# Register-addressed column copies: 24 a step on VectorE and on ScalarE, addresses in four parts, three operand blocks

## The chip, the cores and the metric

The kernel runs on one core of a Trainium2 chip. The metric is the device time of one execution in microseconds (us). A core has a matrix engine (TensorE, PE in the profile; PEld is its weight load), VectorE (DVE), ScalarE (ACT), GpSimd (POOL) and SyncE (SP). Each engine has a sequencer that reads its instructions in order and hands them to the engine; rows of the profile with a q behind the engine's name (DVEq, ACTq) are instructions that the sequencer carries out itself, such as loading registers from memory. Engines wait for each other by semaphores. Matrix results land in PSUM, from where VectorE or ScalarE take them; everything else works in SBUF, 128 partitions wide.

## The reference

One layer of a graph network on 12,500 nodes and 212,500 edges, sorted by destination, in float32; then a residual addition and a layer norm:

```python
msg_in = jnp.concatenate([nodes[row], nodes[col], edge_features], axis=-1)
messages = _mlp(msg_in, mW1, mb1, mW2, mb2)          # relu(x @ W1 + b1) @ W2 + b2
aggregated = jax.ops.segment_sum(messages, col, num_segments=nodes.shape[0])
upd_in = jnp.concatenate([nodes, aggregated], axis=-1)
x = _layernorm(x + _mlp(upd_in, uW1, ub1, uW2, ub2), axis=-1)
```

Node features are 64 wide, edge features 32, hidden layers 128. `row` is the source of an edge, `col` its destination.

## The kernel before

Edges go in 554 groups (G) of 384 (GE, three tiles of 128). Since edges are sorted, a group's destinations lie in a window of 32 nodes. One step of the main loop (L718) works on three groups at once, in a pipeline, all of it one run of TensorE instructions that waits once, at its first, and signals once, at its last:

- `turn` of group k (L423) transposes the group's gathered source features and its one-hot matrix of destinations (`own_s`, 128 x 96) into PSUM. ScalarE evacuates that into the operand block `own_st` (L440).
- `hidden` of group k - 2 (L448) multiplies `own_st`, which also holds the edge features, with weights and the window's projected destinations (`own_wm`). ScalarE applies the ReLU (L464).
- `sums` of group k - 4 (L474) sums the messages by destination. VectorE adds them to `own_agg` (L495) and the counts to a row of `own_xc` (L496), at a column that a register gives.

PSUM buffers alternate by k, so TensorE's step k + 2 waits for what ScalarE and VectorE did after step k.

The source features come in two ways. Most groups are **gathered**: GpSimd issues three indirect DMAs a group (L184), 16 steps ahead, into a ring of 20 buffers; a gather waits for ScalarE's evacuation of the group that had the buffer, and for copies of that step. The other groups (the table COPIED) are **copied**: all nodes also lie transposed in SBUF (`own_xc`, a node is a column of 64 partitions), and VectorE and ScalarE copy one column after another to the group's place in `own_st`, in the steps ahead of the group's own. Each copy is an instruction of 64 x 4 bytes (L599 on VectorE, L601 on ScalarE) whose address stands in a register. Copying starts at step 18 (BEGIN). COLS columns a step are copied, so a copied group is ready every 384 / COLS steps.

The addresses lie in SBUF as whole numbers, eight steps' worth a buffer (`index`, made by L563). `registers(k, part)` (L565) makes the load into registers (TENSOR_LOAD, L578), `fetch(part)` (L585) the copies that use them. VCOLS and ACOLS give the parts: before, VectorE has parts of 12 and 8, ScalarE one of 16. The order in which these calls stand in the loop is the order on each engine:

- VectorE's load of 12 stands right ahead of the additions (called from `add` by way of the list `between`), its copies of 12 behind them; then come the one-hot of group k + 6 (L412), the load of 8 and the copies of 8.
- ScalarE's load of 16 for step k + 1 stands behind the copies of step k, thus ahead of step k + 1's evacuation and ReLU; the 16 copies come behind the ReLU.
- Every fourth step, VectorE also loads 4 registers with the columns of the sums (L371).

`own_st` has four blocks (BLOCKS) of four groups. `inputs(b)` (L355) has SyncE load a block's edge features (192 KB); it waits for the step that last read the block, as does the first copy of a group on each engine (L603).

Some 23 times, when a stretch of 512 nodes has all its sums, an `update` of those nodes runs through the steps in six parts (L500 to L548): two products, a ReLU, two products, statistics and scaling.

Of the kernel before, what the change touches and what calls it, by code (L numbers as in the profile page):

```python
# [32 lines left out]
G = (E + GE - 1) // GE  # L33
SB = 4
AHEAD = 16
RING = AHEAD + 4
BLOCKS = 4
NW = 2 * SB
COUNT = 96
NH = 3  # L40
# [9 lines left out]
TIMES = 4  # L50
BEGIN = 18
CHECKED = 8
VCOLS = (12, 8)
ACOLS = (16,)
COLS = sum(VCOLS + ACOLS)
SPAN = 8
STREAMS = ()
# [4 lines left out]
def tiles_of(g):  # L62

    n = min(GE, E - g * GE)
    return [min(P, n - j * P) for j in range((n + P - 1) // P)]
# [27 lines left out]
for _, rate, _ in STREAMS:  # L93
    BY_ROWS.append([])
    while True:
        last = BEGIN + (P * (len(BY_ROWS[-1]) + 1) - 1) // rate + ROW_LEAD
# [7 lines left out]
class Own:  # L104
# [4 lines left out]
    def __init__(self, nc, ctx):  # L109
        def on(name, *shape, of=nc.sbuf_tensor):  # L110
            return ctx.enter_context(of(name, list(shape), F32)).ap()

        self.s = [on(f"own_s{i}", P, TG, D + W) for i in range(RING)]
        self.st = [on(f"own_st{i}", P, SB * GE) for i in range(BLOCKS)]
        self.wm = [on(f"own_wm{i}", P, H) for i in range(NW)]
# [14 lines left out]
def ordered(ctx: ExitStack, tc: tile.TileContext, a, own, ok):  # L130
# [28 lines left out]
    def after(first, *others):  # L159

        tc.declare_no_dep(first.ins, group="quiet", reason="waits for the last of a step")
        for i in others:
            tc.add_manual_dep(
                first.ins, i.ins.name,
                mybir.DependencyInfo(mybir.DependencyClass.Sync, mybir.DependencyReason.DATA),
                reason="the kernel's own rings",
            )
        return first
# [73 lines left out]
    def bit(k):  # L242

        nodes = [NEAR_NODES + (N - NEAR_NODES) * i // BITS for i in (k, k + 1)]
        tiles = [first + (NT - first) * i // BITS for i in (k, k + 1)]
        nc.sync.dma_start(src_sb[:, slice(*tiles)], a["src"][:, slice(*tiles)])
        nc.sync.dma_start(xc[:D, slice(*nodes)], a["xT"][:, slice(*nodes)])
        rest(nodes[0], nodes[1] if k < BITS - 1 else NP)

    def zeroed(k):  # L250

        n0, n1 = (NP * i // BITS for i in (k, k + 1))
        nc.vector.memset(agg[:, n0:n1], 0.0)
# [101 lines left out]
    def inputs(b):  # L355
        if b * SB >= G:
            return
        c0, c1 = b * SB * GE, min(E, (b + 1) * SB * GE)
        efs_by[b] = nc.sync.dma_start(own.st[b % BLOCKS][D + W :, : c1 - c0], a["efT"][:, c0:c1])
        after(efs_by[b], *([hidden_by[(b - BLOCKS + 1) * SB - 1]] if b >= BLOCKS else []))  # L360

    def columns(g):
        t, c = own.st[g // SB % BLOCKS], (g % SB) * GE
        return t, c, sum(tiles_of(g))
# [13 lines left out]
    def projected(c):  # L378

        base, n = TABLE[c]  # L380
        ps = ups.tile([H, CH], F32, name="u_ps").rearrange("p (n h) -> p n h", n=4)
        for j in range(n):
            nc.tensor.matmul(ps[:, j], xc[: D + 1, base + j * P :][:, :P], w1b,  # L383
                             start=True, stop=True)
        t = rowp.tile([P, 4, H], F32, name="t")
        nc.scalar.activation(t[:, :n], ps[:, :n], AF.Copy)  # L386
        written.append(after(nc.sync.dma_start(
            by_dst[base : base + n * P, :].rearrange("(n p) h -> p n h", n=n), t[:, :n])))
# [34 lines left out]
    def turn(g, ps):  # L423
# [11 lines left out]
        def copy(step):  # L435
# [4 lines left out]
                after(nc.scalar.activation(t[r, c : c + n], xt[r, :n], AF.Copy), step))]  # L440
            if g >= BLOCKS * SB:
                after(copies[0], hidden_by[g - BLOCKS * SB])
            copy_by[g] = copies
# [30 lines left out]
    def sums(g, ps):  # L474
        h, s = own.h[g % NH], own.s[g % RING]
        sizes = tiles_of(g)
        sg = ps[2][:, : TIMES * W].rearrange("p (t w) -> p t w", w=W)
        counted = ps[2][0:1, TIMES * W :][:, :W]
        did = []
        for j, p in enumerate(sizes):  # L480
            did.append(nc.tensor.matmul(  # L481
                sg, h[:p, j, :],
                s[:p, j, D:].unsqueeze(1).to_broadcast([p, TIMES, W]),
                start=j == 0, stop=j == len(sizes) - 1))
        for j, p in enumerate(sizes):
            did.append(nc.tensor.matmul(counted, own.one[:p], s[:p, j, D:],  # L486
                                        start=j == 0, stop=j == len(sizes) - 1))

        def add(step):
            sums_by[g] = step  # L490
            at = bass.ds(starts.pop(g), W)
            count = xc[COUNT : COUNT + 1, at]
            if between:
                between.pop()()
            a = after(nc.vector.tensor_tensor(agg[:, at], sg[:, 0, :], agg[:, at], ALU.add), step)  # L495
            return [a, after(nc.vector.tensor_tensor(count, counted, count, ALU.add), step)]  # L496

        return did, [*relu_by[g], *copy_by[g]], add
# [60 lines left out]
    def addresses(i):  # L559

        if i in indices:
            t = indices[i][:, : min(SPAN * COLS, GE * len(COPIED) - i * SPAN * COLS)]
            nc.vector.tensor_scalar(t, t, 4.0, float(own.at), ALU.mult, ALU.add)  # L563

    def registers(k, *parts):  # L565

        i, n = divmod(k - BEGIN, SPAN)
        if i < 0:
            return
        all_parts = [*((ET.DVE, c) for c in VCOLS), *((ET.Activation, c) for c in ACOLS)]  # L570
        for part in parts:
            engine, count = all_parts[part]
            c0 = (k - BEGIN) * COLS + sum(c for _, c in all_parts[:part])
            count = min(count, GE * len(COPIED) - c0)
            if count <= 0:
                return
            b = c0 - i * SPAN * COLS
            _, v = nc.values_load_multi_w_load_instructions(  # L578
                indices[i][0:1, b : b + count], engines=[engine],
                min_val=own.at, max_val=own.at + 4 * (N - 1),  # L580
                skip_runtime_bounds_check_because="a source is one of the nodes",
            )
            held[part] = engine, c0, v
# [129 lines left out]
    for n in range(len(STREAMS)):  # L713
        row_indexes(n, 0)
    made = summed = 0
    between, held, last = [], {}, {}

    for k in range(G):  # L718
        if k < BITS:
            bit(k)  # L720
            if k + 2 < BITS:
                zeroed(k + 2)
        if 1 < k < len(TABLE):
            projected(k)
        if k == CHECKED:
            addresses(0)
            for n in range(len(STREAMS)):
                row_addresses(n, 0)
            combined()
            ordered_edges()  # L730
            early.close()
            up = ctx.enter_context(tc.tile_pool(name="upd", bufs=2))
        if k % SB == 2:
            inputs(k // SB + 2)
        if k % SB == 1:
            places(k // SB + 1)
        if k < G - SHORT:
            between.append(lambda: registers(k, 0))
            step((turn, k), *([(hidden, k - 2)] if k > 1 else []),
                 *([(sums, k - 4)] if k > 3 else []))  # L740
            made, summed = max(0, k - 1), max(0, k - 3)
            if between:
                between.pop()()
        else:

            step((turn, k))
            for _ in range(2):
                if summed < made:
                    step((sums, summed))
                    summed += 1  # L750
            for _ in range(2):
                if made <= k:
                    step((hidden, made))
                    made += 1
            registers(k, 0)
        fetch(0)
        window(k + SB)
        for n in range(len(STREAMS)):
            row_numbers(n, k)
            row_fetch(n)  # L760
        onehot(k + LEAD)
        marks_by[k] = [copy_by[k][-1]]
        if k < G - 1:
            for part in range(1, len(VCOLS + ACOLS)):
                if part != len(VCOLS):
                    registers(k, part)
                fetch(part)
                if part >= len(VCOLS) and ET.Activation in last:
                    marks_by[k].append(last[ET.Activation])
            if k + 1 < G - 1:  # L770
                registers(k + 1, len(VCOLS))
            if k >= BEGIN and (k - BEGIN) % SPAN == 0:
                indexes((k - BEGIN) // SPAN + 1)
            if k >= BEGIN and (k - BEGIN) % SPAN == SPAN - 2:
                addresses((k - BEGIN) // SPAN + 1)
        if k + AHEAD < G:
            gather(k + AHEAD)
# [333 lines left out]
```

## Time and profile before

| | |
|---|---|
| median of 3 runs | 1914.63 us (1913.1 to 1914.86) |
| the profiled execution | 1914.16 us |
| its span, first to last instruction | 1912.4 us |
| granted TensorE clock, mean | 0.972 |
| busy: PE, PEld | 1324.3 us (69%), 1170.6 us (61%) |
| busy: DVE, ACT, POOL | 1251.4 us (65%), 1325.2 us (69%), 1431.7 us (75%) |

Times with a decimal point in views of the trace are us from the span's start. In the waits, "A <- B" says that A's engine stood idle until B released it; the numbers are us in total, the count, and the longest. In a timeline the columns are start, duration (of a merged row, up to its last end), engine, line, operation, tiles, shape and count, and in brackets the idle time ahead of it. In views of one line, three numbers with slashes are the shortest, the median and the longest duration in ns.

### The profile page before, as it was taken

To read this page: it belongs to the slowest core of one execution; us is meant where nothing else is said; L and a number is where in the kernel's file an instruction comes from. 1 tells how busy PE (TensorE), PEld (TensorE's weight loads), DVE (VectorE), ACT (ScalarE), POOL (GpSimd) and SP (SyncE) were. 2 spreads that over 40 slices of the span, in tenths; PEclk is the share of its full clock that TensorE was granted. 3 is DMA by queue.
4 is the path that set the end of the run, shared out by engine and by line. 5 is a ranking of instruction groups with operands and counts; after the bars stand their busy time and mean duration, and the time that the engine had idled before them with its cause. 6 is when DMAs were issued, how large, how long until landed. Compare 5 with 4: busy or idle time off the path is not lost. (4 is left out here: it accounts for less than half of the span.)

```text
span 1912.4 us, 56586 instructions
## 1 busy us (share of the span) xinstructions
PE 1324.3 (69%) x12323; PEld 1170.6 (61%) x12323; DVE 1251.4 (65%) x12584; ACT 1325.2 (69%) x9559; POOL 1431.7 (75%) x1521
## 2 busy tenths in 40 slices
PE   5877777767767766676666776766766766667677
PEld 4766666666656655665655665655656655556566
DVE  4347777766666666676766766666667666676662
ACT  4468787766767767776767776776676677676662
POOL 7777777777777777777777777777777777777774
PEclk9889999989999999999999999999999999999998
DMA  5532222222222222222222212222222222222221
GB/s 141 139 97 64 53 50 52 49 49 48 45 53 52 46 52 48 49 49 48 53 48 48 50 44 53 52 46 52 48 50 48 51 47 52 45 53 48 49 50 25
DMA packets 113836, 105.15 MB, mean 55 GB/s; under 512 B 52115, under 2 KB 83488, under 8 KB 113488
## 3 DMA queue, kind: packets, MB, share of 16 engines
q0 software_dynamic: 48448, 49.68, 13.6%
q1 hardware_dynamic: 64196, 51.29, 9.7%
q8 instruction: 104, 1.70, 0.4%
q14 instruction: 244, 2.00, 0.3%
q10 hardware_dynamic: 844, 0.48, 0.1%
HBM read 91.68 MB, written 9.62 MB: 53 GB/s over the span
## 5 line engine op out<-in xcount | busy, mean ns | idle before, releaser
L184 POOL DMA_INDIRECT own_s<-in_x,src_sb x1514 | 1430.9, 945 | 462.5 <-issue 261.5
L599 DVE COPY own_st<-own_xc 64x4 uint8 x10460 | 896.5, 191 | 27.7 <-DMA by_dst<-t 3.5
L601 ACT ACTIVATE own_st<-own_xc 64x4 uint8 x8356 | 847.3, 195 | 2.9 <-DMA by_dst<-t 2.9
L429 PE MATMUL own_ps<-own_ident,own_s 128*96 128x128 f32 x1661 | 289.0, 284 | 540.4 <-DMA own_s<-in_x,src_sb 355.6
L440 ACT ACTIVATE own_st<-own_ps 96x384 f32<-96x384 f32 (+1 forms) x554 | 268.6, 485 | 506.7 <-PE own_ps L486 483.7
L429 PEld LDWEIGHTS own_ps<-own_ident,own_s 128*96 128x96 f32 x1661 | 164.3, 129 | 602.0 <-ACT own_h L464 445.0
L481 PE MATMUL own_ps<-own_s,own_h 128*128 128x128 f32 x3322 | 478.6, 282 | 1.3 <-ACT own_h L464 0.6
L495 DVE TENSOR_TENSOR own_agg<-own_ps,own_agg 128x32 f32 x554 | 106.3, 192 | 567.1 <-PE own_ps L486 386.4
L453 PE MATMUL own_ps<-own_wm,own_st 128*128 128x128 f32 x3322 | 476.5, 281 | 0.0
L481 PEld LDWEIGHTS own_ps<-own_s,own_h 128*128 128x128 f32 x3322 | 431.1, 198 | 2.8 <-ACT own_h L464 1.6
L453 PEld LDWEIGHTS own_ps<-own_wm,own_st 128*128 128x128 f32 x3322 | 428.6, 197 | 1.3 <-issue 0.5
L464 ACT ACTIVATE own_h<-own_ps 128x384 f32<-128x384 f32 x553 | 264.8, 479 | 21.2 <-PE own_ps L453 20.0
L486 PE MATMUL own_ps<-own_s,own_one 128*1 128x32 f32 x3322 | 189.1, 194 | 0.0
L486 PEld LDWEIGHTS own_ps<-own_s,own_one 128*1 128x1 f32 x3322 | 113.8, 83 | 69.4 <-issue 5.7
L412 DVE TENSOR_TENSOR own_s<-iota,dlc 128x96 f32<-128x96 f32 x554 | 137.3, 248 | 0.7
L496 DVE TENSOR_TENSOR own_xc<-own_ps,own_xc 1x32 f32 x554 | 102.1, 184 | 31.9 <-PE u_ps L507 13.2
L383 PE MATMUL u_ps<-w1b,own_xc 65*128 65x128 f32 x196 | 31.8, 310 | 32.0 <-DMA own_xc<-in_xT 12.7
L383 PEld LDWEIGHTS u_ps<-w1b,own_xc 65*128 65x128 f32 x196 | 26.8, 211 | 35.0 <-issue 20.3
L519 PE MATMUL u_ps<-same,own_xc 65*128 65x64 f32 (+1 forms) x196 | 39.5, 283 | 0.4 <-ACT u L512 0.4
L386 ACT ACTIVATE t<-u_ps 128x512 f32<-128x512 f32 (+1 forms) x25 | 14.7, 588 | 36.2 <-DMA by_dst<-t 20.0
L521 PE MATMUL u_ps<-u,u 128*128 128x64 f32 (+1 forms) x196 | 38.2, 277 | 0.0
L519 PEld LDWEIGHTS u_ps<-same,own_xc 65*128 65x128 f32 (+1 forms) x196 | 29.9, 192 | 2.5 <-ACT u L512 1.0
(60 smaller groups left out, 264.4 us busy)
## 6 DMA issues: line engine op xcount, KB each, us to landing
own_st<-in_efT SPq DMA_DIRECT2D x138, 192.0 KB
own_s<-in_x,src_sb POOLq DMA_INDIRECT x1514
own_wm<-by_dst SPq DMA_DIRECT2D x554, 16.0 KB
by_dst<-t SPq DMA_DIRECT2D x24, 256.0 KB
out<-o SPq DMA_DIRECT2D x24, 128.0 KB
own_xc<-in_xT SPq DMA_DIRECT2D x12, 179.2 KB
index<-in_src_copied SPq DMA_DIRECT2D x65, 1.1 KB
dlc_i<-in_dst_cols SPq DMA_DIRECT2D x1, 807.0 KB
```

The source lines that it names most:

```text
L184: nc.gpsimd.indirect_dma_start(out=s[:p, j, :D], out_offset=None, in_=x[:, :], in_offset=bass.IndirectOffsetOnAxis(ap=src_sb[:p, g * TG + ...
L412: places_by[g] = nc.vector.tensor_tensor(own.s[g % RING][:, :, D:], iota.unsqueeze(1).to_broadcast([P, TG, W]), dlc[:, g * TG : (g + 1) * ...
L429: nc.tensor.transpose(xt[:, j * P : j * P + p], sides[g] if g in sides and j == TG - 1 else s[:p, j, :], ident[:p, :p])
L440: after(nc.scalar.activation(t[r, c : c + n], xt[r, :n], AF.Copy), step))]
L453: nc.tensor.matmul(pre[:p, j, :], t[:, c + j * P : c + j * P + p], wm[g % NW], start=True, stop=True)
L464: relu_by[g] = [nc.scalar.activation(h, pre, AF.Relu)]
L481: did.append(nc.tensor.matmul(sg, h[:p, j, :], s[:p, j, D:].unsqueeze(1).to_broadcast([p, TIMES, W]), start=j == 0, stop=j == len(sizes) - 1))
L486: did.append(nc.tensor.matmul(counted, own.one[:p], s[:p, j, D:], start=j == 0, stop=j == len(sizes) - 1))
L495: a = after(nc.vector.tensor_tensor(agg[:, at], sg[:, 0, :], agg[:, at], ALU.add), step)
L496: return [a, after(nc.vector.tensor_tensor(count, counted, count, ALU.add), step)]
L599: by[engine] = nc.vector.tensor_copy(o, x_at)
L601: by[engine] = nc.scalar.activation(o, x_at, AF.Copy)
```

## The change

Both engines copy 24 columns a step (COLS 48 instead of 36), and both take their addresses in parts of 12, 4, 4 and 4. VectorE's load of 12 moves behind the additions; ScalarE's first load is now that of the same step and stands behind the ReLU. `own_st` has three blocks.

```diff
-BLOCKS = 4
+BLOCKS = 3
...
-VCOLS = (12, 8)
-ACOLS = (16,)
+VCOLS = (12, 4, 4, 4)
+ACOLS = (12, 4, 4, 4)
...
             count = xc[COUNT : COUNT + 1, at]
-            if between:
-                between.pop()()
             a = after(nc.vector.tensor_tensor(agg[:, at], sg[:, 0, :], agg[:, at], ALU.add), step)
...
-    between, held, last = [], {}, {}
+    held, last = {}, {}
...
         if k < G - SHORT:
-            between.append(lambda: registers(k, 0))
             step((turn, k), *([(hidden, k - 2)] if k > 1 else []),
                  *([(sums, k - 4)] if k > 3 else []))
             made, summed = max(0, k - 1), max(0, k - 3)
-            if between:
-                between.pop()()
         else:
...
-            registers(k, 0)
+        registers(k, 0)
+        if k < G - 1:
+            registers(k, len(VCOLS))
         fetch(0)
         window(k + SB)
...
-            if k + 1 < G - 1:
-                registers(k + 1, len(VCOLS))
```

VectorE in a plain step of the middle of the program, before; the row without names (ISA) computes the address of the addition behind it, and TENSOR_LOAD is a load of addresses:

```order
L578 TENSOR_LOAD index
L495 ISA
L495 TENSOR_TENSOR own_agg<-own_ps,own_agg 128x32
L496 ISA
L496 TENSOR_TENSOR own_xc<-own_ps,own_xc 1x32
L599 COPY own_st<-own_xc 64x4 x12
L412 TENSOR_TENSOR own_s<-iota,dlc 128x3x32
L578 TENSOR_LOAD index
L599 COPY own_st<-own_xc 64x4 x8
```

The same place in the changed program, from the addition on (line numbers are two lower there):

```order
L493 TENSOR_TENSOR own_agg<-own_ps,own_agg 128x32
L494 ISA
L494 TENSOR_TENSOR own_xc<-own_ps,own_xc 1x32
L576 TENSOR_LOAD index
L597 COPY own_st<-own_xc 64x4 x12
L412 TENSOR_TENSOR own_s<-iota,dlc 128x3x32
L576 TENSOR_LOAD index
L597 COPY own_st<-own_xc 64x4 x4
L576 TENSOR_LOAD index
L597 COPY own_st<-own_xc 64x4 x4
L576 TENSOR_LOAD index
L597 COPY own_st<-own_xc 64x4 x4
```

The first load, of 12, now stands behind the two additions and right ahead of its copies; three loads of 4 have taken the place of one of 8.

ScalarE in a plain step, before, from one load to the next:

```order
L578 TENSOR_LOAD index
L440 ACTIVATE own_st<-own_ps 96x384
L464 ACTIVATE own_h<-own_ps 128x384
L601 ACTIVATE own_st<-own_xc 64x4 x16
L578 TENSOR_LOAD index
```

And in the changed program:

```order
L440 ACTIVATE own_st<-own_ps 96x384
L464 ACTIVATE own_h<-own_ps 128x384
L576 TENSOR_LOAD index
L599 ACTIVATE own_st<-own_xc 64x4 x12
L576 TENSOR_LOAD index
L599 ACTIVATE own_st<-own_xc 64x4 x4
L576 TENSOR_LOAD index
L599 ACTIVATE own_st<-own_xc 64x4 x4
L576 TENSOR_LOAD index
L599 ACTIVATE own_st<-own_xc 64x4 x4
```

The load that stood ahead of the evacuation, where ScalarE waits for TensorE, now stands behind the ReLU, and is of 12; the other 12 addresses come in three parts of 4, each right ahead of its copies.

## The prediction

> **What bounds the kernel now.** I read the page first, for the engines' busy time and the costliest groups; then the table of waits, since no engine is busy throughout; then the timeline of the two engines in question.
>
> ```profile
> span 1912.4 us, 56586 instructions
> ...
> L184 POOL DMA_INDIRECT own_s<-in_x,src_sb x1514 | 1430.9, 945 | 462.5 <-issue 261.5
> ```
> ```profile
> DVE own_agg L495 <- PE own_ps L486: 386.4, 324, 6.7
> ...
> POOL own_s L184 <- issue: 261.5, 858, 0.3
> POOL own_s L184 <- DMA own_s<-in_x,src_sb: 173.7, 570, 0.3
> DVE own_agg L495 <- DVE own_st L599: 77.4, 130, 1.0
> ```
> ```profile
> 1063.67 0.94 POOL L184 DMA_INDIRECT own_s<-in_x,src_sb  x1 [0.30 <-issue]
> 1064.92 0.94 POOL L184 DMA_INDIRECT own_s<-in_x,src_sb  x1 [0.30 <-DMA own_s<-in_x,src_sb]
> ```
>
> GpSimd is busy for 75% only, yet it never pauses longer than 0.3 us: that is its fixed distance between two gathers, whatever name stands at it. So a gather costs (1430.9 + 462.5) / 1514 = 1.25 us, and all of them cost 1893 us of a span of 1912.4. **The gathers are the bound.** VectorE waits mostly for TensorE, which waits for gathers. But in 130 steps VectorE waited for nothing but its own last copies, with nothing running on it. That row is where the change will hurt. Here is such a step, from one addition to the next:
>
> ```profile
> 1062.15 0.19 DVE L495 TENSOR_TENSOR own_agg<-own_ps,own_agg 128x32 f32 x1 [0.90 <-DVE mv L529]
> 1062.37 0.18 DVE L496 TENSOR_TENSOR own_xc<-own_ps,own_xc 1x32 f32 x1
> 1062.59 0.94 DVE L599 COPY own_st<-own_xc 64x4 uint8 x12
> 1063.44 0.24 DVE L412 TENSOR_TENSOR own_s<-iota,dlc 128x96 f32<-128x96 f32 x1
> 1063.61 0.68 DVE L599 COPY own_st<-own_xc 64x4 uint8 x8
> 1064.85 0.19 DVE L495 TENSOR_TENSOR own_agg<-own_ps,own_agg 128x32 f32 x1 [0.55 <-DVE own_st L599]
> ```
> ```profile
> L578 DVEq TENSOR_LOAD <-index x2: 593/720/846, 1062.8 to 1063.7; - x2
> ```
>
> The second view is that of the line that loads addresses, in this one step: a load of 8 registers at 1062.8 takes 0.593 us, one of 12 at 1063.7 takes 0.846 us. It ends at 1064.55, and the addition behind it starts at 1064.85, although the copies had been handed out long before. The sequencer does nothing else while it loads. The step lasts 2.70 us with only some 2.0 us of work on the engine: **VectorE's floor is its sequencer**, and 0.593 + 0.846 = 1.44 us of it are loads. Today gathers leave room above that floor.
>
> **The change part by part.** *Fewer gathers.* 48 columns a step instead of 36 make 65 copied groups of 384 instead of 49. That removes 48 gathers; at 1.25 us they are worth 60 us. In a loaded step GpSimd then needs 3 x (1 - 48/384) x 1.25 = 3.28 us. The copies last 65 x 384 / 48 = 520 steps instead of 49 x 384 / 36 = 523. Whoever takes longer than 3.28 us a step becomes the new bound.
>
> *VectorE.* Its loads go from 12 + 8 to 12 + 4 + 4 + 4, its copies from 20 to 24. What a load of 4 more costs can be read, because every fourth step has one (L371, the addresses of the sums):
>
> ```profile
> L371 DVEq TENSOR_LOAD <-start_i x139: 340/343/812, 10.5 to 1882.2; - x139
> ```
> ```profile
> 1150.21 0.19 DVE L495 TENSOR_TENSOR own_agg<-own_ps,own_agg 128x32 f32 x1 [1.01 <-DVE own_st L599]
> ...
> 1153.34 0.19 DVE L495 TENSOR_TENSOR own_agg<-own_ps,own_agg 128x32 f32 x1 [0.97 <-DVE own_st L599]
> ```
> ```profile
> L371 DVEq TENSOR_LOAD <-start_i x1: 347/347/347, 1151.8 to 1151.8; - x1
> ```
>
> This step has that load, again VectorE waited for itself alone, and it lasts 3.13 us: 0.43 more than 2.70, for a load of 0.347. So in a plain step:
> - the load of 8 becomes one of 4: 0.593 - 0.343 = 0.25 less;
> - two more loads of 4: 2 x 0.43 = 0.86 more;
> - four more copies handed over: in the step above 8 of them lie between the end of the load at 1062.8 + 0.593 and the next load at 1063.7, so at most 0.3 / 8 = 0.04 each, part of which is the pause between two loads. I take 0.03, so 0.12; the bounds are 0 and, if 20 copies had made up all of 2.70 - 1.44, 0.25;
> - the load of 12 moves from ahead of the addition to behind it. It stays in the same chain: 0.
>
> The last point needs the question whether the sequencer can run the load while the addition still waits for TensorE. The nearest rows are at the start, on ScalarE:
>
> ```profile
> 12.12 0.60 ACT L386 ACTIVATE t<-u_ps 128x512 f32<-128x512 f32 x1 [2.16 <-PE u_ps L383]
> 12.12 0.47 ACTq L301 DMA_DIRECT2D w2t<-in_mW2T  x1
> ```
>
> The sequencer's own instruction starts only when the activation ahead of it has stopped waiting. So the load begins with the addition at the earliest. Queued behind it are the 24 copies and the one-hot of the step; the next addition comes behind all of those. TensorE waits for the addition two steps on.
>
> Plain step: 2.70 - 0.25 + 0.86 + 0.12 = **3.43 us**. Per step come on top: 0.43 / 4 = 0.11 for L371; and VectorE's share of the updates and of the address arithmetic:
>
> ```profile
> L543 DVE TENSOR_SCALAR o<-u_ps,mv,rstd 128x64 f32<-128x64 f32 (+1 forms) x98 | 27.0, 337 | 1.0
> L563 DVE TENSOR_SCALAR index<-index 1x288 int32<-1x288 int32 x66 | 22.2, 336 | 0.1
> L528 DVE BATCH_NORM_STATS2 stats<-u_ps 128x6 f32<-128x64 f32 (+1 forms) x98 | 20.4, 208 | 5.3 <-PE u_ps L521 5.3
> L529 DVE BATCH_NORM_AGGREGATE mv<-stats 128x2 f32<-128x6 f32 (+1 forms) x98 | 17.8, 182 | 3.5
> ```
>
> L528 and L529 stand in the chain, 38 us; of L543's 27 I count 10, as a load can run beside them: 48 / 520 = 0.09. L563 runs every eighth step, 0.336 / 8 = 0.04, half of it beside loads: 0.02. The average is 3.43 + 0.11 + 0.09 + 0.02 = **3.65 us**, above GpSimd's 3.28. The bound moves from GpSimd to VectorE, and GpSimd will wait for ring space.
>
> *ScalarE* gets 24 copies for 16, and its load of 16 in front becomes 12 behind the ReLU and three of 4.
>
> ```profile
> 1066.12 0.49 ACT L440 ACTIVATE own_st<-own_ps 96x384 f32<-96x384 f32 x1
> 1066.51 0.48 ACT L464 ACTIVATE own_h<-own_ps 128x384 f32<-128x384 f32 x1
> 1066.88 1.62 ACT L601 ACTIVATE own_st<-own_xc 64x4 uint8 x16
> 1068.48 0.49 ACT L440 ACTIVATE own_st<-own_ps 96x384 f32<-96x384 f32 x1
> ```
> ```profile
> L578 ACTq TENSOR_LOAD <-index x523: 313/1021/1340, 90.2 to 1852.7; - x175
> ```
>
> Evacuation and ReLU take 0.76, 16 copies 1.60, so 0.10 each; 16 registers take 1.02, the shortest load (4, the last one) 0.313, so 12 take about 0.78. If the load starts with the evacuation, copies begin at 0.9 and the step takes 0.9 + 2.4 = 3.3; the short loads run beside the copies ahead of them. If it starts only with the ReLU (0.39) and each short load shows 0.1, it is 3.8. I take 3.3, which is nearest to the rows of L386 and L301: no cost, hidden under VectorE's 3.65; without that cover it would be 0.02 over GpSimd's 3.28.
>
> *TensorE* has the same work in a step, about 2.1 us:
>
> ```profile
> 1063.04 0.53 PE L429 MATMUL own_ps<-own_ident,own_s 128*96 128x128 f32 x3
> ...
> 1064.85 0.34 PE L486 MATMUL own_ps<-own_s,own_one 128*1 128x32 f32 x6
> ```
>
> *Three operand blocks.* The edge load on SP (L359) waits for a step one before the step that issues it instead of five before, and the first column of a group waits for a step two back. The landed data is needed eight steps later, some 28 us; that hides it at no cost. Were it late by 1 us each time, 139 loads would cost 139 us.
>
> **Sum.** Loaded stretch before, by the copies' first and last start:
>
> ```profile
> L599 DVE COPY own_st<-own_xc x10460: 148/156/424, 99.1 to 1857.2; 64x4 uint8 x198
> ```
>
> That is 1758 us for 523 steps, 3.36 each. The profiled execution took 1914.2 us; 156 of it lie outside the stretch. Outside come three more steps at ScalarE's shortest period of 2.36 (7 us), less the waits for the last gathers, which now land long before:
>
> ```profile
> 1860.72 0.51 PE L429 MATMUL own_ps<-own_ident,own_s 128*96 128x128 f32 x3 [1.39 <-DMA own_s<-in_x,src_sb]
> ...
> 1894.31 0.50 PE L429 MATMUL own_ps<-own_ident,own_s 128*96 128x128 f32 x3 [1.58 <-DMA own_s<-in_x,src_sb]
> ```
>
> These are the first and the last of five, 5 us in all. That leaves 158. Inside: 520 x 3.65 = 1898. Together **2056 us**, 142 above the profiled execution, which is 0.5 below the median of 1914.63. I give 2055.
>
> **Rivals.**
> - *The loads hide* (12 in 100). If copies can be handed on while a load runs, VectorE's step falls to its own work, 24 copies at 0.07 and the additions, some 2.3 us. GpSimd stays the bound, and 48 gathers less give 1914 - 60 = **1854**. For it: GpSimd never waits today. Against it: 77.4 us of VectorE waiting for itself, and the 0.43 for one more load. [...]
> - *ScalarE becomes the bound* (10 in 100), if its load starts with the ReLU: some 3.75 a step, 520 x 3.75 + 158 = **2108**. It decides above 3.65.
> - *The edge loads come late* (2 in 100): 2055 + 139, near **2190**. SP's queue behind a waiting L359 also holds the windows of four steps on.
>
> **How the numbers follow.** The forecast has 76 in 100. Its unknown terms give, all low (copies handed over for nothing, updates 0.03), 3.45 a step and 1952; all high (0.25, 0.13, 0.04), 3.84 and 2155. Not all lie at one end, so I take 1960 to 2140, which also holds the ScalarE case. A measurement here can tell about 0.2%, 4 us. Faster than that: the first rival, 12 in 100. Slower: 86. Within: 2, should the loads hide in part.
>
> **What would show it.** Right: GpSimd waits far over 0.3 us for ScalarE's copies or the transposes; VectorE's additions wait for L599's copies (now L597) instead of for TensorE, about 3.4 us apart in plain steps; between additions there is a gap ahead of the first copy and ahead of each set of four. Wrong: gathers still 1.25 us apart throughout; or ScalarE without idle time and VectorE waiting for TensorE.

## The result and the profile after

| | before | after |
|---|---|---|
| median | 1913.99 us (1913.1 to 1914.86, 4 runs) | 2067.63 us (2063.42 to 2072.74, 4 runs) |
| ratio | | 1.0804, 95% interval 1.0779 to 1.0829 |
| profiled execution, span | 1914.16 us, 1912.4 us | 2072.74 us, 2070.9 us |
| granted TensorE clock | 0.972 | 0.943 |

The change makes the kernel 8% slower. The page after, its head and the costliest groups of the three engines in question (busy time, mean ns of one, idle time ahead of them):

```profile
span 2070.9 us, 65565 instructions
...
L184 POOL DMA_INDIRECT own_s<-in_x,src_sb x1466 | 1385.0, 945 | 612.1 <-ACT own_st L440 188.3
L597 DVE COPY own_st<-own_xc 64x4 uint8 x12480 | 1118.9, 187 | 469.5 <-issue 440.2
L599 ACT ACTIVATE own_st<-own_xc 64x4 uint8 x12480 | 1249.4, 193 | 47.1 <-DVE own_xc L494 38.3
```

The table of waits after (total us, times, longest in us):

```profile
DVE own_st L597 <- issue: 440.2, 909, 1.1
PEld own_ps L429 <- ACT own_h L464: 408.3, 254, 2.7
...
POOL own_s L184 <- ACT own_st L440: 188.3, 228, 4.1
POOL own_s L184 <- issue: 184.6, 604, 0.4
POOL own_s L184 <- ACT own_st L599: 164.8, 401, 1.5
ACT own_st L440 <- PE own_ps L486: 153.0, 178, 9.2
...
DVE own_agg L493 <- PE own_ps L486: 62.3, 36, 7.0
```

There are 48 gathers less, as the change promised, but GpSimd now pauses up to 4.1 us for ScalarE, where no pause between gathers was over 0.3 us before. VectorE's wait for TensorE fell from 386.4 us to 62.3 us. Its idle time stands ahead of its own copies, with "issue" as its cause: the engine waits for its own sequencer. A plain step on VectorE after, and the view of the address loads in that step:

```profile
1060.87 0.19 DVE L493 TENSOR_TENSOR own_agg<-own_ps,own_agg 128x32 f32 x1
1061.09 0.18 DVE L494 TENSOR_TENSOR own_xc<-own_ps,own_xc 1x32 f32 x1
1062.01 1.02 DVE L597 COPY own_st<-own_xc 64x4 uint8 x12 [0.74 <-issue]
1062.94 0.24 DVE L412 TENSOR_TENSOR own_s<-iota,dlc 128x96 f32<-128x96 f32 x1
1063.11 0.66 DVE L597 COPY own_st<-own_xc 64x4 uint8 x8
1063.94 0.38 DVE L597 COPY own_st<-own_xc 64x4 uint8 x4 [0.17 <-issue]
1064.23 0.18 DVE L493 TENSOR_TENSOR own_agg<-own_ps,own_agg 128x32 f32 x1
```
```profile
L576 DVEq TENSOR_LOAD <-index x4: 341/344/847, 1061.1 to 1063.5; - x4
```

The step lasts 3.36 us instead of 2.70. Between the additions and the first copy VectorE stands idle for 0.74 us while its sequencer loads 12 registers for 0.847 us. The second addition has 0.18 us of work to cover that, no more. The last four copies again wait 0.17 us for their load.

That VectorE sets the step, and not ScalarE, is not to be read from the names in the waits. Most of TensorE's waiting after is put down to ScalarE's ReLU (L464; 408.3 us in the table above). Three views of one such wait, TensorE's weight loads, VectorE's count addition and ScalarE:

```profile
1087.18 0.20 PEld L486 LDWEIGHTS own_ps<-own_s,own_one 128*1 128x1 f32 x6
1088.59 0.28 PEld L429 LDWEIGHTS own_ps<-own_ident,own_s 128*96 128x96 f32 x3 [1.21 <-ACT own_h L464]
```
```profile
1088.34 0.18 DVE L494 TENSOR_TENSOR own_xc<-own_ps,own_xc 1x32 f32 x1
```
```profile
1087.95 0.48 ACT L464 ACTIVATE own_h<-own_ps 128x384 f32<-128x384 f32 x1
```

The ReLU ends at 1088.43 and the weight load starts at 1088.59. VectorE's addition ends at 1088.52, 0.07 us ahead. Between the first and the last copy TensorE's step begins after a wait of more than 0.3 us 405 times; in 401 of them it starts 0.07 us after the end of VectorE's count addition, while the distance to the last ReLU goes from 0 to 5 us. Before the change, 53 of 368 such waits ended in that way. The constant distance points to the true releaser; the name in the row is inferred, and here it is not the one that was waited for.

### The profile page after: what moved, and what is told of

Its sections match the earlier page's. It is cut to its first block, busy times and chain, and to the rows that moved or that the text cites. A ratio compares the mean times of both kernels' runs of the same rounds, so it can differ in the third digit from the quotient of the medians.

```text
span 2070.9 us, 65565 instructions
## 1 busy us (share of the span) xinstructions
PE 1379.6 (67%) x12323; PEld 1218.9 (59%) x12323; DVE 1445.0 (70%) x14603; ACT 1738.6 (84%) x13683; POOL 1385.8 (67%) x1473
## 5 line engine op out<-in xcount | busy, mean ns | idle before, releaser
L184 POOL DMA_INDIRECT own_s<-in_x,src_sb x1466 | 1385.0, 945 | 612.1 <-ACT own_st L440 188.3
L597 DVE COPY own_st<-own_xc 64x4 uint8 x12480 | 1118.9, 187 | 469.5 <-issue 440.2
L599 ACT ACTIVATE own_st<-own_xc 64x4 uint8 x12480 | 1249.4, 193 | 47.1 <-DVE own_xc L494 38.3
L429 PE MATMUL own_ps<-own_ident,own_s 128*96 128x128 f32 x1661 | 298.3, 291 | 619.8 <-ACT own_h L464 390.6
L429 PEld LDWEIGHTS own_ps<-own_ident,own_s 128*96 128x96 f32 x1661 | 171.1, 133 | 683.8 <-ACT own_h L464 408.3
L481 PE MATMUL own_ps<-own_s,own_h 128*128 128x128 f32 x3322 | 500.6, 291 | 2.8 <-ACT own_h L464 2.3
L453 PE MATMUL own_ps<-own_wm,own_st 128*128 128x128 f32 x3322 | 494.3, 288 | 0.0
L481 PEld LDWEIGHTS own_ps<-own_s,own_h 128*128 128x128 f32 x3322 | 452.8, 207 | 5.0 <-ACT own_h L464 3.9
L453 PEld LDWEIGHTS own_ps<-own_wm,own_st 128*128 128x128 f32 x3322 | 446.0, 204 | 1.7 <-issue 0.5
L440 ACT ACTIVATE own_st<-own_ps 96x384 f32<-96x384 f32 (+1 forms) x554 | 265.9, 480 | 169.1 <-PE own_ps L486 153.0
L464 ACT ACTIVATE own_h<-own_ps 128x384 f32<-128x384 f32 x553 | 264.5, 478 | 22.8 <-PE own_ps L453 21.2
L493 DVE TENSOR_TENSOR own_agg<-own_ps,own_agg 128x32 f32 x554 | 106.7, 193 | 99.0 <-PE own_ps L486 62.3
L533 ACT ACTIVATE rstd<-mv,eps 128x4 f32<-128x4 f32 (+1 forms) x25 | 7.4, 297 | 46.4 <-DVE mv L527 46.4
L504 PE MATMUL u_ps<-own_agg,wc 128*128 128x512 f32 (+1 forms) x50 | 28.2, 647 | 25.1 <-DVE own_agg L493 25.1
```

Of the source, the lines that this page charges most:

```text
L184: nc.gpsimd.indirect_dma_start(out=s[:p, j, :D], out_offset=None, in_=x[:, :], in_offset=bass.IndirectOffsetOnAxis(ap=src_sb[:p, g * TG + ...
L429: nc.tensor.transpose(xt[:, j * P : j * P + p], sides[g] if g in sides and j == TG - 1 else s[:p, j, :], ident[:p, :p])
L453: nc.tensor.matmul(pre[:p, j, :], t[:, c + j * P : c + j * P + p], wm[g % NW], start=True, stop=True)
L464: relu_by[g] = [nc.scalar.activation(h, pre, AF.Relu)]
L481: did.append(nc.tensor.matmul(sg, h[:p, j, :], s[:p, j, D:].unsqueeze(1).to_broadcast([p, TIMES, W]), start=j == 0, stop=j == len(sizes) - 1))
L597: by[engine] = nc.vector.tensor_copy(o, x_at)
```

## The experiments

Theory: VectorE's sequencer makes the loss, by the number of its loads. Rivals: the three blocks, the new place of the loads, ScalarE's 24 copies in four parts, or VectorE's four more copies by themselves. The runs e1, e2, e3 and e6 stand against 1916.79 us of the kernel before (1915.78 to 1918.34), e11 and e12 against 1917.21 us (1916.4 to 1917.64).

### e1: four blocks

On the changed kernel:

```diff
-BLOCKS = 3
+BLOCKS = 4
```

> The changed kernel with four operand blocks again, nothing else. My theory: the block count is hidden and costs nothing, so the time stays at the changed kernel's 2067 us, within 8. Rival (edge loads come late with three blocks, or copies wait for a block): it drops by the price of those waits, to 1930 if they were the whole of the loss, and SyncE's edge loads (L359) no longer hold up TensorE.

Measured: 2061.92 us (2057.01 to 2070.89), ratio 1.0772, interval 1.0746 to 1.0798, which overlaps with the changed kernel's (1.0779 to 1.0829). What one block less costs, 0.3%, is not clear of the noise.

### e2: only the new places

On the changed kernel, with the numbers of before:

```diff
-BLOCKS = 3
+BLOCKS = 4
-VCOLS = (12, 4, 4, 4)
-ACOLS = (12, 4, 4, 4)
+VCOLS = (12, 8)
+ACOLS = (16,)
```

> The kernel before (parts 12 and 8, 16; 36 columns; four blocks) with the loads in their new places alone: VectorE's 12 behind the additions, ScalarE's 16 behind the ReLU. My theory: VectorE's sequencer has the same chain, 2.70 us in a plain step, so gathers remain the bound at 3.37 a step: 1914 us, within 6; ScalarE's plain step grows from 2.36 to about 2.7, still covered. Rival (the place costs, since the load no longer runs while the addition waits for TensorE): 0.85 us a step on VectorE, some 0.2 to 0.4 of it over the cover, 2000 us or more.

Measured: 1916.81 us (1913.42 to 1918.45, 10 runs), ratio 1.000, interval 0.999 to 1.0009. Two waits of this run:

```profile
DVE own_st L597 <- issue: 354.7, 562, 1.1
POOL own_s L184 <- issue: 269.5, 884, 0.3
```

VectorE now has the gap ahead of its copies here too, 562 times, and it costs nothing: the gathers still come at their fixed distance of 0.3 us. Here 354.7 us of waiting on an engine off the bound are no loss.

### e3: the new numbers in the old places

On the kernel before:

```diff
-BLOCKS = 4
+BLOCKS = 3
-VCOLS = (12, 8)
-ACOLS = (16,)
+VCOLS = (12, 4, 4, 4)
+ACOLS = (12, 4, 4, 4)
```

> The changed kernel (48 columns, parts 12, 4, 4, 4, three blocks) with the loads in their old places: VectorE's 12 ahead of the additions, ScalarE's 12 for the next step behind its copies. My theory: place is not the cost, the number of loads is; VectorE's plain step stays 3.38 to 3.43 us and the time 2045 to 2085. Rival (place): the step falls by up to the load's 0.85 us, gathers bound again, 1855 to 1900.

Measured: 2090.25 us (2 runs, 2082.7 and 2097.81), ratio 1.0904, interval 1.0858 to 1.095, just over what was expected. The loss comes with the numbers, not with the places. The new places even save a little: 1% lies between this run's ratio and the changed kernel's, and their intervals do not meet. In this run VectorE waits for TensorE more:

```profile
DVE own_agg L495 <- PE own_ps L486: 236.3, 228, 7.1
```

TensorE in turn waits for VectorE here as well: 411 of its 414 waits of over 0.3 us end 0.07 us after VectorE's count addition. So VectorE still sets the step; what the 236.3 us consist of stays open.

### e6: VectorE's parts alone

On the changed kernel, ScalarE with one load of 16 as before, but in its new place (40 columns in all, four blocks):

```diff
-BLOCKS = 3
+BLOCKS = 4
-ACOLS = (12, 4, 4, 4)
+ACOLS = (16,)
```

> VectorE with 12, 4, 4, 4 as in the changed kernel, ScalarE with one load of 16 and 16 copies (40 columns, four blocks). My theory (VectorE alone is the bound): plain step 3.38, average 3.65 to 3.7, 518 steps and 160 us outside: 2050 to 2080, and ScalarE waits for TensorE in most steps. Rival (ScalarE's 24 copies and four loads make the loss, or a good part of it): ScalarE's step is back to 2.7 us and the time near 1900 to 1950.

Measured: 2058.3 us (2054.71 and 2061.9), ratio 1.0737, interval 1.0714 to 1.076. The waits of this run:

```profile
DVE own_st L597 <- issue: 434.3, 921, 1.1
ACT own_st L440 <- PE own_ps L486: 365.2, 382, 9.4
```

VectorE's gap is that of the changed kernel (440.2 us, 909 times), ScalarE waits for TensorE more than twice as long as there (153.0 us), and nearly all of the loss is there. VectorE's part of the change makes it alone.

### e11: more loads, no more copies

On the kernel before; VectorE copies 20 columns as before, with five loads for two:

```diff
-VCOLS = (12, 8)
+VCOLS = (4, 4, 4, 4, 4)
```

> The kernel before with VectorE's addresses in five parts of 4 (20 columns a step as before, five loads for two; ScalarE, blocks and the places of the loads as before). Theory (each load holds VectorE's sequencer for about 0.34 us and another 0.1 us before it goes on, and none of this lies beside the copies): the plain step takes 2.70 - 0.593 - 0.846 + 5 x 0.34 + 2 or 3 x 0.09 = 3.2 to 3.35 us by VectorE, over the gathers' 2 x 1.25 + 0.3, and the time goes up to 1950 to 2080 us where the kernel before takes 1914. Rival (what costs is the four more copies a step, or ScalarE, and loads lie beside copies): 1910 to 1925, as before. If this run's copies stand still between one another without a wait, as in the runs of the second chip, its time says nothing on either.

Measured: 1999.1 us (1998.32 to 2006.39), ratio 1.0426, interval 1.0409 to 1.0444. Two consecutive steps on VectorE, the first view, and the loads of the second step:

```profile
1011.04 0.19 DVE L495 TENSOR_TENSOR own_agg<-own_ps,own_agg 128x32 f32 x1 [0.37 <-DVE own_st L599]
...
1013.37 0.38 DVE L599 COPY own_st<-own_xc 64x4 uint8 x4 [0.49 <-issue]
1013.91 0.43 DVE L599 COPY own_st<-own_xc 64x4 uint8 x4 [0.16 <-issue]
1014.63 0.19 DVE L495 TENSOR_TENSOR own_agg<-own_ps,own_agg 128x32 f32 x1 [0.30 <-DVE own_st L599]
...
1016.61 0.38 DVE L599 COPY own_st<-own_xc 64x4 uint8 x4 [0.16 <-issue]
1017.14 0.38 DVE L599 COPY own_st<-own_xc 64x4 uint8 x4 [0.16 <-issue]
1017.87 0.19 DVE L495 TENSOR_TENSOR own_agg<-own_ps,own_agg 128x32 f32 x1 [0.35 <-DVE own_st L599]
```
```profile
L578 DVEq TENSOR_LOAD <-index x5: 339/343/346, 1015.1 to 1017.3; - x5
```

The second step is plain: 3.24 us, 0.54 more than 2.70, with not one copy more. Five loads of 0.343 are 1.72 us, the two before were 1.44: 0.28 of the 0.54 is time in loads. The other 0.26 are three more pauses, 0.09 each. In the whole run 425 of TensorE's 428 waits of over 0.3 us end 0.07 us after VectorE's count addition. The rival (copies make the loss, loads lie beside them) expected no change and falls. The first of the two steps is 3.59 us long; its gap of 0.49 us is told of at the end.

### e12: the change without VectorE's part

On the changed kernel; VectorE as before the change, all else as changed (44 columns):

```diff
-VCOLS = (12, 4, 4, 4)
+VCOLS = (12, 8)
```

> The changed kernel with VectorE's addresses back in 12 and 8 (20 columns on VectorE, 24 on ScalarE in 12, 4, 4, 4; 44 columns; three blocks; the loads in their new places). Theory (VectorE's four loads make the loss): VectorE's plain step is back at 2.70 us, ScalarE's at 3.17 us hides or binds slightly, and the two gathers a step become fewer; the time lies at 1865 to 1950 us where the kernel before takes 1914: near 1870 if ScalarE's step hides, near 1950 if ScalarE binds at 3.17 x 520 + 158 + its extras. Rival (24 columns on ScalarE cost by themselves as much as the change): 2040 to 2080.

Measured: 1876.04 us (1875.21 to 1876.27), ratio 0.9785, interval 0.9769 to 0.9801: faster than both kernels. The page's head and the group of the gathers, with two consecutive gathers of the timeline:

```profile
span 1874.1 us, 62625 instructions
```
```profile
L184 POOL DMA_INDIRECT own_s<-in_x,src_sb x1481 | 1403.2, 947 | 452.8 <-DMA own_s<-in_x,src_sb 198.3 <-issue 117.7 <-ACT own_st L599 78.6
```
```profile
1064.47 0.95 POOL L184 DMA_INDIRECT own_s<-in_x,src_sb  x1 [0.30 <-DMA own_s<-in_x,src_sb]
1065.73 0.95 POOL L184 DMA_INDIRECT own_s<-in_x,src_sb  x1 [0.30 <-issue]
```

The gathers are the bound again: (1403.2 + 452.8) / 1481 = 1.25 us each, 1856 of 1874.1 us. There are 33 fewer than before, 33 x 1.25 = 41 us, and 1917.21 - 1876.04 is 41. Of TensorE's 355 waits of over 0.3 us only 8 end with VectorE's count addition. So ScalarE's 24 copies in four parts, the places and the three blocks bring what the gathers saved are worth, in full, as long as VectorE keeps its two loads.

### Runs that settle little

Six runs came from series in which the kernel before itself took 2510 and 2536 us, at granted clocks of 0.75 to 0.85 in these runs, so that none of their ratios can be set beside the others. They were the changed kernel with `VCOLS = (12, 12)`, twice; the kernels of e12 and e11; and, twice, the kernel before with `VCOLS = (12, 10)`, `ACOLS = (12, 12)` and three blocks.

> The changed kernel with VectorE's 24 addresses in two loads of 12 instead of 12, 4, 4, 4; still 48 columns and three blocks. My theory: three loads of 4 with their pauses (3 x 0.43) become one load of 12 (0.85 and a pause), 0.36 us a step less: plain step 3.02, average about 3.3, near GpSimd's 3.28: 1880 to 1910. Rival (24 copies on VectorE are too many as such, however their addresses come): 2030 or more.

> VectorE with 12 and 8 (20 copies), ScalarE with 24 copies in 12, 4, 4, 4 as changed (44 columns, three blocks). My theory: VectorE's plain step is 2.70 again, 3.0 on average; gathers bound at 3.32 a step with 33 fewer of them: 1873, at most 1890 if ScalarE's step (about 3.2) shows now and then. Rival (ScalarE's four loads are a bound as well): 1930 or more, with TensorE waiting for ScalarE.

> The kernel before, with VectorE's same 20 addresses in five loads of 4 instead of 12 and 8; no other change. My theory: loads of 1.72 us instead of 1.44 and three more pauses of 0.085 make a plain step of 3.23, and with 0.3 on average for the rest 3.5, over GpSimd's 3.37: 1950 to 2000. Rival (loads hide, and the loss came from the added copies): 1915.

> A version meant to beat both: loads in their old places, VectorE 12 and 10, ScalarE 12 and 12 (46 columns, three blocks). My theory: VectorE's plain step is 2.9 (2 registers more are 0.13, 2 copies 0.07), 3.2 on average; ScalarE's 3.1; gathers bound at 3.30 with 39 fewer of them, 49 us less: 1866, within 12. Rival (VectorE at 3.3 or more a step): 1890 to 1920.

> The kernel of e8_46 once more (VectorE 12 and 10, ScalarE 12 and 12, old places, three blocks), on a chip on which the kernel before takes its 1914 us. Theory: gathers bound at 3.30 a step, 39 fewer of them: 1866, within 12, 2.5% faster than the kernel before. Rival (VectorE at 3.3 or more a step, or ScalarE): 1890 to 1920.

> The kernel of e4_ve12_12 once more (the changed kernel with VectorE's 24 addresses in two loads of 12), on a chip on which the kernel before takes its 1914 us. Theory (the number of loads is the cost): plain step 3.02, average 3.3: 1880 to 1910, below the kernel before. Rival (24 copies on VectorE are too many as such): 2030 or more.

Measured: 2520.09 us and 2555.39 us for 12 + 12 (ratios 1.0041, interval 1.0017 to 1.0065, and 1.0078, 1.0048 to 1.0109); 2530.56 us for the kernel of e12 (1.008, 1.0054 to 1.0106); 2537.7 us for that of e11 (1.0102, 1.0072 to 1.0132); 2893.73 and 2889.59 us for 46 columns (1.1511, 1.1482 to 1.1539, and 1.1372, 1.1328 to 1.1416). That these ratios don't carry over is seen in e11 and e12, the same kernels as two of them: 1.0426 and 0.9785 there. One wait of the second run with 12 + 12:

```profile
ACT own_st L599 <- issue: 302.4, 569, 1.2
```

ScalarE's copies stand still between one another 569 times without a wait; in the changed kernel that cause has 1.6 us in all. Its loads take their usual time (a median of 0.31 us for 4), and the cause was not found. So whether VectorE with 12 + 12 would beat e12 where the kernel before takes 1914 us stays open.

The loss with 46 columns goes with its loads. The address loads of the second such run, then four in a row on VectorE, two steps with 12 and 10 each:

```profile
L578 DVEq TENSOR_LOAD <-index x1036: 849/1843/3084, 170.6 to 2831.7; - x173
L578 ACTq TENSOR_LOAD <-index x1035: 314/2579/3032, 170.4 to 2824.9; - x173
```
```profile
L578 DVEq TENSOR_LOAD <-index x1: 853/853/853, 1060.7 to 1060.7; - x1
L578 DVEq TENSOR_LOAD <-index x1: 1077/1077/1077, 1062.5 to 1062.5; - x1
L578 DVEq TENSOR_LOAD <-index x1: 2736/2736/2736, 1064.0 to 1064.0; - x1
L578 DVEq TENSOR_LOAD <-index x1: 2302/2302/2302, 1067.7 to 1067.7; - x1
```

The loads of one step are short and those of the next long, all through the run and in the first such run too. A step has 46 whole numbers of 4 bytes, 184 bytes. So VectorE's parts begin at a multiple of 16 bytes from the start of the buffer in one step and 8 bytes past one in the next; on ScalarE, whose parts begin after 22 numbers, the steps are the other way round. Sorted by that place, the median load of 12 takes 0.85 us on VectorE and 0.79 on ScalarE at a multiple of 16, and 2.74 and 2.60 us beside one. In the other runs every part has a multiple of 4 numbers, and every load begins at a multiple of 16. By this VectorE's floor with 46 columns is, as an estimate, half of the four loads' 6.97 us and the 1.26 us that 2.70 leaves beside its loads: 4.7 us a step, over the changed kernel's 3.69. So by this estimate 46 columns in this layout would not beat e12 where the kernel before takes 1914 us either. No run changed the place alone.

## Why the prediction was right, point by point

Forecast 2055 us, measured 2067.63; the mechanism is the one that was forecast, and its terms come out as follows.

- **The bound moves from the gathers to VectorE's sequencer.** Right, by the waits above and by e6 and e12: with VectorE's loads the loss is there without ScalarE's part, without them it is gone with ScalarE's part.
- **The load of 8 for one of 4 (-0.25) and two more loads at 0.43 each (+0.86).** Right. e11 measures the same price by itself: three more loads, 0.54 a step, half of it the loads and half the pauses (five times 0.43, less the loads of 12 and 8 with a pause of 0.09 each, is 0.53). The figure of 0.43 for a load of 0.347, read from one step with L371, was what the forecast rested on.
- **Four more copies handed over (+0.12).** Too high by 0.04. Over all steps with four loads and nothing else the median distance between additions is 3.39 us, 0.15 more than e11's 3.24. One load of 12 and three of 4 are 1.88 us against 1.72 (+0.16), one pause is gone (-0.09), so four copies cost 0.08. The plain step was forecast at 3.43, which is too long by those 0.04.
- **What comes on top in other steps (0.22).** Too low: it was 0.30. The copies of the changed kernel on VectorE, by their first and last start:

```profile
L597 DVE COPY own_st<-own_xc x12480: 149/158/425, 97.5 to 2015.4; 64x4 uint8 x199
```

  That is 1918 us for 520 steps, 3.69 each (before: 3.36). By the distances between additions, L371 costs 0.42 a time (0.11 a step, as forecast) and L563 (now L561) 0.14 (0.02, as forecast). A step of an update with statistics is 1.40 longer, one with scaling 1.19: 23 x 2.59 = 60 us, 0.11 a step for 0.09. The difference is L543 (now L541): 17 of its 27 us were held to lie beside a load, but the load of 12 that could lie there has moved behind the additions. In e3, with that load in its old place, a step with scaling is only some 0.35 longer than a plain one. The rest, 0.30 - 0.11 - 0.02 - 0.11 = 0.06 a step, may be pauses of the sequencer, 0.35 us each, that the forecast didn't know (below).
- **The load of 12 moved: 0.** Right for the plain step: 3.41 in e3 with the old places, 3.39 in the changed kernel. (e2's 1.000 alone couldn't show it, as gathers cover VectorE there.) The whole kernel is 1% slower with the old places. Only the sign to look for was named wrongly in one point: VectorE's additions do not wait for its copies (18.7 us in all); with the load behind the additions the gap stands ahead of the first copy, as the same list said.
- **ScalarE hidden, 3.3 a step.** Right, and 3.17 in the step below; steps in which ScalarE did not wait are mostly 3.02 to 3.17. Its timeline after, and the loads of 12 of the two steps that begin at 1065.07 and 1068.36:

```profile
1065.07 0.49 ACT L440 ACTIVATE own_st<-own_ps 96x384 f32<-96x384 f32 x1 [1.34 <-PE own_ps L486]
...
1068.36 0.48 ACT L440 ACTIVATE own_st<-own_ps 32x384 f32<-32x384 f32 x1
1068.86 0.49 ACT L464 ACTIVATE own_h<-own_ps 128x384 f32<-128x384 f32 x1
1069.25 2.38 ACT L599 ACTIVATE own_st<-own_xc 64x4 uint8 x24
1071.53 0.47 ACT L440 ACTIVATE own_st<-own_ps 96x384 f32<-96x384 f32 x1
```

```profile
L576 ACTq TENSOR_LOAD <-index x1: 777/777/777, 1065.1 to 1065.1; - x1
L576 ACTq TENSOR_LOAD <-index x1: 782/782/782, 1067.9 to 1067.9; - x1
```

  Where the evacuation has waited for TensorE, the load of 12 begins with it, as chosen (the first step). Where it stands behind copies, the load begins even earlier, here 0.41 us ahead of the evacuation, and the 24 copies run in one piece right behind the ReLU. The three short loads (0.31 us each) lie beside the copies. So the same four loads that cost VectorE its step cost ScalarE nothing that shows (e12: 1876.04 us with them). On ScalarE a burst of 12 copies lasts 1.2 us, at 0.1 each, longer than the 0.31 us of a load of 4. VectorE's four copies at 0.07 are done in 0.28 us, less than a load of 4 (0.34 us) and its pause. In sum, ScalarE is at work for 3.17 us of such a step, and VectorE for 2.42 us of the plain step shown further up. The rival in which ScalarE binds falls with e6 and e12.
- **Three blocks: 0.** Right within the noise (e1). The rival of late edge loads falls.
- **The loads hide.** Falls: by e11 and by the gap ahead of the first copies, 0.74 us in the median. In the traces of the changed kernel and of e11 no copy that found VectorE idle began while a load ran, and the soonest came 0.08 us after a load's end (0.09 in the changed kernel).
- **Sum.** 520 x 3.69 = 1918, and 2072.7 - 1918 = 155 outside, forecast 158. The miss of 13 us is 0.04 a step too little (21 us), 3 too much outside, and 5 by which the median lies below the profiled execution. That it is so small is in part luck: the plain step was too long by 0.04, the other steps too short by 0.08, and pauses of the sequencer were not known.

## What to carry to other kernels

In this kernel loads into registers, and not only work, set VectorE's floor: 2.70 us a step with two loads, 3.24 with five and not one copy more (e11). So count such loads on the engine's sequencer, at their length plus a pause each (here 0.34 us and 0.09 for a load of 4), and compare with what the bound leaves (here 3.28 us a step for the gathers). Splitting them cost nothing that shows on ScalarE, where each part's work lasts longer than the next load (1.2 us for 12 copies and 0.4 for 4, against 0.31). On VectorE, where four copies last 0.28 us and a load 0.34, two long loads did better than five short ones: 1917.21 us against 1999.1. Lay the list out as in the runs whose loads all begin at a multiple of 16 bytes: a load of 12 took 0.85 us there, and 2.74 us where it began 8 bytes past one. And a change in several parts is to be tried with one part left out: here one of them made the whole loss, and hid a gain of 2%.

## What the runs showed of the hardware beyond that

**A load into registers** takes 0.34 us for 4 and 0.847 for 12 on VectorE in the changed kernel and 0.593 for 8 in the kernel before, by these about 0.063 a register and 0.09 once; in the changed kernel a copy for which VectorE stands idle mostly starts another 0.09 to 0.10 us behind it. These figures are of loads that begin at a multiple of 16 bytes in the buffer. In the two runs with 46 columns, loads that begin 8 bytes past one take 2.74 us for 12 and 2.30 for 10, 0.23 a register, and a load of 10 at a multiple of 16 takes 1.08, longer than one of 12.

**In e11 VectorE's sequencer pauses for some 0.35 us at multiples of 128 instructions.** In the two steps shown under e11 the gap of 0.49 us instead of 0.16 is such a pause, and nothing waited for is named. By the distances between one load and the next, 94 such pauses of 0.33 to 0.38 us can be told in e11's loop, whose 16,712 instructions on VectorE are 130 times 128. Of the 93 distances between them 72 are 126 to 130 instructions, and all lie within 2 of a multiple of 128. In the changed kernel 31 pauses of 0.35 to 0.44 us can be told in the same way, and 26 of the 30 distances between them lie within 4 of a multiple of 128. Those 31 are 11 us, 0.02 a step. Its loop has some 18,200 instructions on VectorE; with a pause at each multiple of 128, not shown there, it would be 142 x 0.35 = 50 us, 0.1 us a step, as an estimate. The 0.06 a step that the other terms don't explain lie between the two. Before the change the gathers covered whatever VectorE lost in this way, as from the first copies to the last none of them came more than 0.3 us behind the one ahead.

In e11 the pauses go with packets of the instruction queue. The profile's pages of the changed kernel and of e11 show that queue (packets, MB, share of time):

```profile
q14 instruction: 314, 2.57, 0.4%
...
q14 instruction: 256, 2.10, 0.3%
```

Nearly all of its packets have 8192 bytes (320 of 327 in the changed kernel's trace), and there is about one for every 128 instructions of VectorE, ScalarE, GpSimd and SyncE: 39,336 in the changed kernel's trace are 307 times 128, 31,938 in e11's are 250 times. In e11 such a packet starts 1.0 to 2.0 us after each of the 94 pauses; at times picked at random one starts so in 12 of 100 cases. The packet comes after the pause, so the sequencer does not wait for this one; what stops it is not shown.
